# Layer 0's chain to the output weights in two streams by head group, and score fills in the 64x64 tile shape

## The chip, the core and the metric

The kernel runs on one core of a Trainium2 chip. The core has a matrix engine (TensorE, PE in the profile; its weight loads are the row PEld), VectorE (DVE), ScalarE (ACT), GpSimd (POOL) and SyncE (SP, which issues nearly all DMAs here). Each engine works through its own instructions in order and waits on semaphores for the others. The metric is the device time of one execution in microseconds (us); less is better. The profile is one execution taken by the hardware profiler.

## What is computed

Sixteen images of 64x64 positions and 256 channels go through two layers, each of which adds to `x` a function of its group norm. Layer 0 is a linear attention with eight heads of 32, layer 1 an attention over a 7x7 neighbourhood with eight heads of 32 and position embeddings.

```python
def _L0_conv_ref(x, w_qkv, w_out):
    q, k, v = to_heads(split(x @ w_qkv))            # 8 heads of 32, n = 4096 positions
    q = softmax(q, over the head's 32) * 32 ** -0.5
    k = softmax(k, over the n positions)
    context = einsum('bhdn,bhen->bhde', k, v)
    out = einsum('bhde,bhdn->bhen', context, q)
    return out @ w_out

def _L1_conv_ref(x, Wq, bq, Wk, bk, Wv, bv, emb0, emb1):
    q, k, v = x @ Wq + bq, x @ Wk + bk, x @ Wv + bv
    kp, vp = 7x7 neighbourhoods of k (plus embeddings) and of v, zeros outside
    attn = softmax(einsum('bhwnd,bhwndk->bhwnk', q, kp))
    return einsum('bhwndk,bhwnk->bhwnd', vp, attn)

x = x + _L0_conv_ref(_gn(x), ...)
x = x + _L1_conv_ref(_gn(x), ...)
```

## The kernel before

All is float32; a float32 matmul goes through PE in two passes and stands as two records in the profile. One image follows the other. The instruction order of PE, ACT, DVE and SP is written out by hand: an engine does its work in the order in which the Python code issues it, and semaphore waits are derived from which tiles an instruction reads and writes. POOL's instructions are placed by the framework.

PSUM, where matmuls write, is held as two double banks `double[0]`, `double[1]` (pd in the profile) and four single banks `single[0]` to `single[3]` (ps).

**Layer 0** (`layer0`, one call per image; its first three steps run at the end of the image before). The positions are cut into 16 blocks `p` of 256 positions, two rows `t` of 128 each.

- `queries_keys(p)` multiplies normalised positions with the query and key weights into a double bank (L588), takes the exponential of all with ACT (L592, tile `eq`), sums the queries of a head with DVE (L595, L597) and divides them with POOL (L598).
- `context(p)` multiplies the exponential of the keys with the raw positions and a column of ones (L606), for both head groups `hg` of four heads, and sums over all 16 blocks in `pc[hg]`, which is `single[hg]`: 256 columns of sums, and the keys' own sum in column 256.
- `turned(p)` transposes the divided queries with DVE into `qv` (L619, two instructions per block).

The loop issues block `p`'s `queries_keys`, then `context(p - 1)`, then `turned(p - 2)`. After the loop comes **the chain** from the contexts to the output weights, for both groups at once: DVE divides and centres the sums into `cc` (reciprocal L644, L645); the transposes of block 15 follow on DVE; PE transposes `cc` into `other[0]`, which is `single[2]` (L653); DVE scales it by the norm's factor into `cT` (L658, two of 128x256); PE multiplies with the value weights into `other[1]`, which is `single[3]` (L663, in 128x32 tiles); DVE scales the product into `ch` (L670); PE multiplies with the output weights into both double banks (L674, in 32x128 tiles); DVE copies the keys' sums out of `pc` (`z`, L682); DVE (L685, two of 128x512) and ACT (L686) copy the output weights to `w4` in SBUF. Then the output matmuls (L709) read `w4` and `qv`: for each of two channel halves, eight strips in four groups of two. The first group writes `single[0]` to `single[3]`, columns 0 to 255, the second the double banks, and so on in turn. A group `i` reads the queries of blocks `4 * i` to `4 * i + 3`. DVE adds each result to `x` (L726, L723) and takes statistics (L522).

**Layer 1** (`local_attention`): eight passes `k` over a head group and a strip of columns (`SEQUENCE`), each in five steps `g` of two row chunks `c`, 40 steps per image. In a step, `scores` multiplies queries and keys in 64x64 tiles (L967) into one of the double banks per chunk, ACT takes the exponential (L976, L979), and in the next step the products with the values follow (L1011). The two double banks alternate, so the scores of a chunk wait for the exponential of the chunk before the last. `blank` (L944) fills the parts of the double bank that no score matmul writes with a large negative number, by four matmuls of bfloat16 constants; it runs for chunks 0 and 1 of passes 0 and 4 alone, that is in steps 0 and 20. Between the steps run jobs that make keys and queries: a matmul into a single bank (L879), then its evacuation by ACT (L755) or DVE (L757).

Of the kernel before, what the change touches and what calls it, by code (L numbers as in the profile page):

```python
# [14 lines left out]
ALU = mybir.AluOpType  # L15
# [4 lines left out]
P = 128  # L20
W = 64
C = 256
# [11 lines left out]
SCALE = HD**-0.5  # L34
# [397 lines left out]
def attention_fast(tc, io, ok):  # L432


    nc = tc.nc
    with ExitStack() as ctx:
# [3 lines left out]
        double = [ps.tile([P, 2, 512], F32, tag=f"pd{i}", name=f"pd{i}") for i in range(2)]  # L440
# [19 lines left out]
        n = Net(tc, cp, io)  # L460
# [19 lines left out]
        bits = cp.tile([P, 2], BF16, tag="bits", name="bits")  # L480
# [16 lines left out]
        def work_tile(name):  # L497
            return work.tile([P, 1024], F32, tag="work", name=name)

        def watch(total, x, w):  # L500
            nc.gpsimd.tensor_tensor(total[:, :w], total[:, :w], x, ALU.add)  # L501
# [10 lines left out]
        def tokens_of(q):  # L512
            return vbuf[q % 2][:, : 8 * (C + 1)].rearrange("p (t c) -> p t c", c=C + 1)

        def load_tokens(b, q, t0=0, t1=8):

            t = tokens_of(q)
            nc.gpsimd.memset(t[:, t0:t1, C : C + 1], 1.0)
            nc.sync.dma_start(t[:, t0:t1, :C], xt[b, q, :, t0:t1])
# [7 lines left out]
        def normalise(xn, x, mean, rstd, s):  # L527
            for k in range(2):
                n.normalise(xn[k][:, strip(s)], x[k][:, strip(s)], mean, rstd, k)
# [42 lines left out]
        def layer0(b, x, xn, mean, rstd, ready, midway=None):  # L572

            mu = None
            pc, other = single[:2], single[2:]
            eq = {}
# [23 lines left out]
                watch(others, z.rearrange("p t h -> p (t h)"), 2 * HEADS)  # L600
                return e

            def context(p):
                for t in range(2):
                    for hg in range(2):
                        nc.tensor.matmul(  # L606
                            pc[hg][:, : C + 1],
                            eq[p][:, t, C + hg * P : C + (hg + 1) * P],
                            tokens_of(p // 4)[:, 2 * (p % 4) + t],
                            start=(p == 0 and t == 0),  # L610
                            stop=(p == 15 and t == 1),
                        )

            def turned(p):

                e = eq.pop(p)
                for t in range(2):
                    T = 2 * p + t
                    nc.vector.transpose(qv[:, :, HD * T : HD * T + HD], e[:, t, :C].rearrange("p (h d) -> p h d", d=HD))  # L619

            for p in range(16 + 1):
                if p < 16:
                    if p % 2 == 0 and p // 2 + 1 < NS and p // 2 + 1 >= ready:
                        normalise(xn, x, mean, rstd, ORDER[p // 2 + 1])
                    eq[p] = queries_keys(p)
                    if p < 3:
                        yield
                if p == 1:
                    mu = n.spread(mean, lambda name: other[1], small, f"{b}")
                if 1 <= p <= 16:  # L630
                    context(p - 1)
                    q = (p - 1) // 4 + 2
                    if q < 4:
                        load_tokens(b, q, 2 * ((p - 1) % 4), 2 * ((p - 1) % 4) + 2)
                if p >= 2:
                    turned(p - 2)
                if p == 9 and midway:
                    fill()

            r = small.tile([P, 2, 1], F32, tag="krz", name=f"krz{b}")  # L640
            z = small.tile([P, 2, 1], F32, tag="kz", name=f"kz{b}")
            cc = work_tile(f"cc{b}")[:, : 2 * C].rearrange("p (a c) -> p a c", c=C)
            for hg in range(2):
                nc.vector.reciprocal(r[:, hg], pc[hg][:, C : C + 1])  # L644
                nc.vector.scalar_tensor_tensor(cc[:, hg], pc[hg][:, :C], r[:, hg], mu, ALU.mult, ALU.subtract)  # L645
            turned(15)


            ct = work_tile(f"ct{b}")
            cT, ch = ct[:, :512].rearrange("p (a c) -> p a c", c=P), ct[:, 512:768]  # L650
            for hg in range(2):
                for k in range(2):
                    nc.tensor.transpose(  # L653
                        other[0][:, (2 * k + hg) * P : (2 * k + hg + 1) * P], cc[:, hg, k * P : (k + 1) * P], n.ident
                    )
            for k in range(2):
                dst = cT[:, 2 * k : 2 * k + 2].rearrange("p a b -> p (a b)")
                nc.vector.tensor_scalar(dst, other[0][:, k * C : (k + 1) * C], rstd[:, k : k + 1], None, ALU.mult)  # L658
            for hg in range(2):
                for k in range(2):  # L660
                    for h in range(4):
                        rows = slice(HD * h, HD * h + HD)
                        nc.tensor.matmul(  # L663
                            other[1][rows, hg * P : (hg + 1) * P].rearrange("p (a d) -> p a d", a=4),
                            n.wqkv_sb[:, k, 2 * C + hg * P + HD * h : 2 * C + hg * P + HD * h + HD],
                            cT[:, 2 * k + hg, rows].unsqueeze(1).to_broadcast([P, 4, HD]),
                            start=(k == 0),
                            stop=(k == 1),
                        )
            nc.vector.tensor_scalar(ch, other[1][:, :C], SCALE, None, ALU.mult)  # L670
            for hg in range(2):
                for h in range(4):
                    rows = slice(HD * h, HD * h + HD)
                    nc.tensor.matmul(  # L674
                        double[h // 2][:, h % 2, hg * C : (hg + 1) * C],
                        ch[rows, hg * P : (hg + 1) * P],
                        n.wout_sb[rows, hg],
                        start=True,
                        stop=True,
                    )  # L680
            for hg in range(2):
                nc.vector.tensor_copy(z[:, hg], pc[hg][:, C : C + 1])  # L682
            w4 = vbuf[0][:, : 8 * C].rearrange("p (h g c) -> p h g c", h=4, g=2)
            for h in range(2):
                nc.vector.tensor_copy(w4[:, h].rearrange("p g c -> p (g c)"), double[0][:, h])  # L685
            nc.scalar.copy(w4[:, 2:4].rearrange("p h g c -> p h (g c)"), double[1])  # L686
            watch(tops, r.rearrange("p a b -> p (a b)"), 2)
            watch(others, z.rearrange("p a b -> p (a b)"), 2)

# [5 lines left out]
            for co in range(2):  # L695
                for i in range(NS // 2):
# [4 lines left out]
                    for h in range(4):  # L701
# [4 lines left out]
                        for hg in range(2):  # L706
                            for a in range(4):
                                rows = slice(HD * a, HD * a + HD)
# [215 lines left out]
        def local_attention(b, x, y, after_scores, read, beside, between, stored):  # L924
# [9 lines left out]
            def blank(hg, pair):  # L934
                for i in range(2):
                    for e in range(2):
                        rows = slice(32 * (2 * i + e), 32 * (2 * i + e) + 32)
                        to = pair[64 * e : 64 * e + 64, i]
                        if hg == 0:
                            to = to.rearrange("p (a w) -> p a w", w=16)[:, :, 8 - 8 * e : 10 - 8 * e]  # L940
                        else:
                            to = to.rearrange("p (a n) -> p a n", a=2)[:, :, 128 - 128 * e : 160 - 128 * e]
                        one = bits[rows, 1:].to_broadcast([32, 64])
                        nc.tensor.matmul(to, nb[rows, :64], one, start=True, stop=True)  # L944

            def scores(k, c):
                hg, t = SEQUENCE[k]
                ps = psum2()
                if k % 4 == 0 and c < 2:
                    blank(hg, ps)  # L950
# [137 lines left out]
            groups = [(k, g) for k in range(8) for g in range(5)]  # L1088
            held, late, before, kept = None, None, None, []
            rs = {}  # L1090
            for step in range(len(groups) + 2):
                new = None
                place(step, FIRST)
                if step < len(groups):
                    k, g = groups[step]
# [5 lines left out]
                if held:  # L1101
                    k, g, es = held
# [11 lines left out]
                if late:  # L1114
                    k, g, es = late
# [5 lines left out]
                if held:  # L1121
                    k, g, es = held
# [4 lines left out]
                if late:  # L1127
                    k, g, es = late
# [16 lines left out]
        with tc.manual_schedule(engines=ORDERED):  # L1145
# [32 lines left out]
            def completed(steps):  # L1178
                while True:
                    try:  # L1180
                        next(steps)
                    except StopIteration as end:
                        return end.value

            lower = layer0(0, x, xn, *gn, 2, midway)
            for b in range(B):
                more = b + 1 < B
                x, xn = halves(b)
                mean, rstd, chain = completed(lower)
# [503 lines left out]
```

## Time and profile before

| | us |
|---|---|
| median of 3 runs | 5272.87 |
| lowest and highest run | 5268.64, 5277.87 |
| profiled execution, its own time | 5278.82 |
| span of its profile | 5276.9 |

The mean granted clock of TensorE is 0.993. The profile is read by groups of instructions and by timeline: a row gives the start, the length, the engine, the line, the operation with its output and inputs (buffer numbers left out), the shape, how many instructions are merged in it, and in brackets the idle time of its engine just before it and who ended it. In the whole execution the groups of the chain and of the fills are:

```profile
L653 PE MATMUL ps<-ident,cc 128*128 128x128 f32 x64 | 14.0, 300 | 13.7 <-DVE cc L645 13.7
L663 PE MATMUL ps<-ct,wqkv 128*32 128x128 f32 x512 | 21.4, 293 | 9.7 <-DVE ct L658 9.7
L674 PE MATMUL pd<-wout,ct 32*128 32x256 f32 x256 | 22.0, 466 | 8.7 <-DVE ct L670 8.7
L709 PE MATMUL ps<-qq,vbuf 32*128 32x256 f32 x4096 | 247.3, 388 | 12.5 <-DVE vbuf L685 12.5
L944 PE MATMUL pd<-bits,nb 32*64 32x64 bf16 x256 | 14.2, 212 | 0.0
```

Here the columns after the bar are the busy time in us, the mean length of one in ns, and the engine's idle time before them in us with what ended it.

### The profile page before, as it was taken

The numbers are of one execution on the slowest core, as the hardware profiler recorded it, in microseconds if no ns is written. First come the engines' busy times: TensorE is split into PE (matmuls) and PEld (weight loads), VectorE is DVE, ScalarE is ACT, GpSimd is POOL, SyncE is SP. The second block draws the span as 40 slices with busy tenths as digits, with TensorE's granted clock in tenths as the row PEclk, the third lists the DMA queues.
The fourth block names the chain that finished last, engine by engine and source line by source line (L and its number), as shares of the span: only waits on it lengthen the run. The fifth ranks groups of instructions, "written<-read, shape, count | busy, mean of one in ns | idle before, by whom it ended". The sixth has DMA issues, their size and how long they took to land. (4 is left out here: it accounts for less than half of the span.)

```text
span 5276.9 us, 175070 instructions
## 1 busy us (share of the span) xinstructions
PE 5114.0 (97%) x76273; PEld 3770.1 (71%) x76273; DVE 2902.3 (55%) x5610; ACT 2629.5 (50%) x3569; POOL 1444.7 (27%) x2630
## 2 busy tenths in 40 slices
PE   7999999999999999999999999999999999999998
PEld 4776767777676776767767677676776767767676
DVE  5464555646546465464655646555465554745545
ACT  1552736527265372653726537174471744727346
POOL 3141231412314123140331403314032140422404
PEclk9999999999999999999999999999999999999999
DMA  5542625436154351543516445164441634417243
GB/s 134 124 119 51 146 64 128 116 56 150 52 131 115 71 135 49 131 117 72 131 49 135 115 80 134 42 138 107 93 122 43 148 95 103 123 43 150 82 92 88
DMA packets 763657, 537.33 MB, mean 102 GB/s; under 512 B 260656, under 2 KB 701616, under 8 KB 761200
## 3 DMA queue, kind: packets, MB, share of 16 engines
q1 hardware_dynamic: 721664, 515.94, 41.1%
q10 hardware_dynamic: 41216, 10.10, 1.2%
q8 instruction: 602, 9.86, 0.8%
q14 instruction: 175, 1.43, 0.1%
HBM read 367.11 MB, written 158.73 MB: 100 GB/s over the span
## 5 line engine op out<-in xcount | busy, mean ns | idle before, releaser
L996 DVE TENSOR_TENSOR e<-e,e 128x384 f32<-128x384 f32 x1024 | 684.3, 698 | 841.5 <-PE ps L1011 364.9
L755 ACT ACTIVATE qq<-ps,bias 32x512 f32<-32x512 f32 (+1 forms) x960 | 699.9, 734 | 812.5 <-DVE bias L750 657.5
L588 PE MATMUL pd<-wqkv,img 128*128 128x512 f32 x2048 | 926.6, 595 | 8.3 <-DVE img L359 8.3
L967 PE MATMUL pd<-qq,kaug 64*64 64x112 f32 (+5 forms) x24192 | 775.4, 267 | 44.0 <-issue 27.4
L967 PEld LDWEIGHTS pd<-qq,kaug 64*64 64x64 f32 x24192 | 673.3, 133 | 180.4 <-issue 92.7
L592 ACT ACTIVATE eq<-pd 128x1024 f32<-128x1024 f32 x256 | 261.9, 1023 | 1063.0 <-PE pd L588 1063.0
L501 POOL TENSOR_TENSOR others<-others,turn 128x9 f32<-128x9 f32 (+2 forms) x384 | 86.5, 225 | 2185.1 <-DVE turn L1056 2184.3
L588 PEld LDWEIGHTS pd<-wqkv,img 128*128 128x128 f32 x2048 | 387.4, 190 | 393.9 <-issue 350.5
L755 ACT ACTIVATE kaug<-ps,bias 32x512 f32<-32x512 f32 (+1 forms) x864 | 554.8, 651 | 181.2 <-PE ps L879 78.0
L979 ACT ACTIVATE e<-pd 128x896 f32<-128x896 f32 (+2 forms) x576 | 465.5, 835 | 227.8 <-PE pd L967 172.6
L595 DVE TENSOR_REDUCE qz<-eq 128x16 f32<-128x512 f32 x256 | 175.6, 686 | 706.5 <-ACT eq L592 706.5
L976 ACT ACTIVATE e<-pd 128x896 f32<-128x896 f32 (+2 forms) x576 | 463.5, 833 | 168.1 <-PE pd L967 114.8
L1011 PE MATMUL ps<-e,vbuf 128*32 128x112 f32 (+1 forms) x18432 | 529.7, 252 | 12.8 <-issue 12.8
L879 PE MATMUL ps<-img,wqn 128*128 128x160 f32 (+2 forms) x3072 | 536.3, 324 | 0.0
L879 PEld LDWEIGHTS ps<-img,wqn 128*128 128x128 f32 x3072 | 472.1, 190 | 55.9 <-DVE r L1063 10.5
L879 PE MATMUL ps<-img,w 128*128 128x512 f32 x1024 | 501.0, 614 | 0.8 <-DVE qq L757 0.3
L1085 POOL TENSOR_TENSOR img<-img,r 128x320 f32<-128x320 f32 (+1 forms) x512 | 489.1, 980 | 5.0
L606 PEld LDWEIGHTS ps<-vbuf,eq 128*128 128x128 f32 x2048 | 386.4, 190 | 144.7 <-issue 99.9
L1011 PEld LDWEIGHTS ps<-e,vbuf 128*32 128x32 f32 x18432 | 388.3, 110 | 140.7 <-issue 103.3
L606 PE MATMUL ps<-vbuf,eq 128*128 128x257 f32 x2048 | 485.1, 381 | 0.0
L831 PE MATMUL pd<-wvn,img 128*128 128x256 f32 x2048 | 468.1, 382 | 4.0 <-DVE hve L354 4.0
L831 PEld LDWEIGHTS pd<-wvn,img 128*128 128x128 f32 x2048 | 383.0, 190 | 67.7 <-issue 15.3
(142 smaller groups left out, 5577.7 us busy)
## 6 DMA issues: line engine op xcount, KB each, us to landing
vbuf<-vpad SPq DMA_DIRECT2D x1152, 96.0 KB
out<-img SPq DMA_DIRECT2D x256, 256.0 KB
vpad<-v SPq DMA_DIRECT2D x112, 512.0 KB
vbuf<-in_xt SPq DMA_DIRECT2D x158, 256.0 KB
img<-in_xc SPq DMA_DIRECT2D x75, 512.0 KB
img<-in_xc SPq DMA_DIRECT2D x106, 256.0 KB
qq<-pos SPq DMA_DIRECT2D x192, 128.0 KB
vbuf<-in_xt SPq DMA_DIRECT2D x60, 384.0 KB
```

Of the source, the lines that this page charges most:

```text
L588: nc.tensor.matmul(ps[:, t], xn[k][:, n0 : n0 + P], n.wqkv_sb[:, k, : 2 * C], start=(k == 0), stop=(k == 1))
L592: nc.scalar.activation(e, ps, AF.Exp)
L606: nc.tensor.matmul(pc[hg][:, : C + 1], eq[p][:, t, C + hg * P : C + (hg + 1) * P], tokens_of(p // 4)[:, 2 * (p % 4) + t], start=(p == 0 an ...
L755: nc.scalar.activation(dst, src, AF.Identity, bias=bias)
L831: nc.tensor.matmul(pi[:, t], x[k][:, n0 : n0 + P], wv[:, k], start=(k == 0 and t == 0), stop=(k == 1 and t == 1))
L879: nc.tensor.matmul(dst, (wq if what == "q" else wk)[:, k, hg * P : (hg + 1) * P], part(x[k]), start=(k == 0 and i == 0), stop=(k == 1 and ...
L967: nc.tensor.matmul(to, kaug[pl][rows, u, 8 * c : 8 * c + 8].rearrange("p r w -> p (r w)"), q, start=True, stop=True,)
L976: nc.scalar.activation(e.rearrange("p (a n) -> p a n", a=2), ps[:, :, : 2 * m], AF.Exp)
L979: nc.scalar.activation(e.rearrange("p (x r) -> p x r", r=hi - lo), src, AF.Exp)
L996: nc.vector.tensor_tensor(part, part, rows_of(hg, c - 1, before, r0, 8 * c), ALU.add)
L1011: nc.tensor.matmul(dst, stationary, pr, **flags)
L1085: nc.gpsimd.tensor_tensor(yv, xv, by_rows(add[:, :, a - w0 : e - w0], xv), ALU.add)
```

## The change

In the chain, each step is split by head group, and the two groups' steps are issued in turn. The contexts of blocks 14 and 15 are issued first for group 0, then for group 1. The transposed sums of group 1 go to `double[0]`, and the value products of group 1 to `single[2]`, so that each group has banks of its own. Scaling and `ch` become instructions of 128 columns: four and two instead of two and one of 256. The transposes of blocks 14 and 15 and the two copies of the keys' sums are issued behind the copies of the output weights. The dictionary of exponential tiles keeps its entries.

In `blank`, the four matmuls take 64 rows of constants instead of 32 and so stand in 64x64 tiles; the value that they write is twice as large.

```diff
-            def context(p):
+            def context(p, groups=(0, 1)):
                 for t in range(2):
-                    for hg in range(2):
+                    for hg in groups:
...
-                e = eq.pop(p)
+                e = eq[p]
...
-                    context(p - 1)
+                    context(p - 1, (0,) if p >= 15 else (0, 1))
...
-                if p >= 2:
+                if 2 <= p < 16:
                     turned(p - 2)
...
+            context(14, (1,))
+            context(15, (1,))
...
-            for hg in range(2):
+            flipped = other[0], double[0][:, 0]
+            products = other[1], other[0]
+
+            def centred(hg):
                 nc.vector.reciprocal(r[:, hg], pc[hg][:, C : C + 1])
                 nc.vector.scalar_tensor_tensor(cc[:, hg], pc[hg][:, :C], r[:, hg], mu, ALU.mult, ALU.subtract)
-            turned(15)
+            def flip(hg):
                 for k in range(2):
+                    nc.tensor.transpose(flipped[hg][:, k * P : (k + 1) * P], cc[:, hg, k * P : (k + 1) * P], n.ident)
+            def scaled(hg):
+                for k in range(2):
+                    nc.vector.tensor_scalar(
+                        cT[:, 2 * k + hg], flipped[hg][:, k * P : (k + 1) * P], rstd[:, k : k + 1], None, ALU.mult
                     )
-            for k in range(2):
-                dst = cT[:, 2 * k : 2 * k + 2].rearrange("p a b -> p (a b)")
-                nc.vector.tensor_scalar(dst, other[0][:, k * C : (k + 1) * C], rstd[:, k : k + 1], None, ALU.mult)
-            for hg in range(2):
+            def valued(hg):
...
-            nc.vector.tensor_scalar(ch, other[1][:, :C], SCALE, None, ALU.mult)
-            for hg in range(2):
+            def weights(hg):
...
-            for hg in range(2):
-                nc.vector.tensor_copy(z[:, hg], pc[hg][:, C : C + 1])
+            centred(0)
+            flip(0)
+            centred(1)
+            scaled(0)
+            flip(1)
+            valued(0)
+            scaled(1)
+            nc.vector.tensor_scalar(ch[:, :P], products[0][:, :P], SCALE, None, ALU.mult)
+            valued(1)
+            weights(0)
+            nc.vector.tensor_scalar(ch[:, P:], products[1][:, :P], SCALE, None, ALU.mult)
+            weights(1)
             w4 = vbuf[0][:, : 8 * C].rearrange("p (h g c) -> p h g c", h=4, g=2)
             for h in range(2):
                 nc.vector.tensor_copy(w4[:, h].rearrange("p g c -> p (g c)"), double[0][:, h])
             nc.scalar.copy(w4[:, 2:4].rearrange("p h g c -> p h (g c)"), double[1])
+            turned(14)
+            turned(15)
+            for hg in range(2):
+                nc.vector.tensor_copy(z[:, hg], pc[hg][:, C : C + 1])
...
-                        rows = slice(32 * (2 * i + e), 32 * (2 * i + e) + 32)
+                        rows = slice(64 * i, 64 * i + 64)
...
-                        one = bits[rows, 1:].to_broadcast([32, 64])
+                        one = bits[rows, 1:].to_broadcast([64, 64])
                         nc.tensor.matmul(to, nb[rows, :64], one, start=True, stop=True)
```

More of the change, by code (lines that the diff above doesn't have):

```diff
@@ L642, in layer0 @@
             cc = work_tile(f"cc{b}")[:, : 2 * C].rearrange("p (a c) -> p a c", c=C)
-            for hg in range(2):
+            ct = work_tile(f"ct{b}")
+            cT, ch = ct[:, :512].rearrange("p (a c) -> p a c", c=P), ct[:, 512:768]
+            flipped = other[0], double[0][:, 0]
+            products = other[1], other[0]
+            def centred(hg):
                 nc.vector.reciprocal(r[:, hg], pc[hg][:, C : C + 1])
                 nc.vector.scalar_tensor_tensor(cc[:, hg], pc[hg][:, :C], r[:, hg], mu, ALU.mult, ALU.subtract)
-            turned(15)
-            ct = work_tile(f"ct{b}")
-            cT, ch = ct[:, :512].rearrange("p (a c) -> p a c", c=P), ct[:, 512:768]
-            for hg in range(2):
+            def flip(hg):
                 for k in range(2):
-                    nc.tensor.transpose(
-                        other[0][:, (2 * k + hg) * P : (2 * k + hg + 1) * P], cc[:, hg, k * P : (k + 1) * P], n.ident
-                    )
-            for k in range(2):
-                dst = cT[:, 2 * k : 2 * k + 2].rearrange("p a b -> p (a b)")
-                nc.vector.tensor_scalar(dst, other[0][:, k * C : (k + 1) * C], rstd[:, k : k + 1], None, ALU.mult)
-            for hg in range(2):
+                    nc.tensor.transpose(flipped[hg][:, k * P : (k + 1) * P], cc[:, hg, k * P : (k + 1) * P], n.ident)
[3 more added lines that the diff above has]
+                        cT[:, 2 * k + hg], flipped[hg][:, k * P : (k + 1) * P], rstd[:, k : k + 1], None, ALU.mult
+                    )
+            def valued(hg):
                 for k in range(2):
@@ L663, in layer0 @@
                         nc.tensor.matmul(
-                            other[1][rows, hg * P : (hg + 1) * P].rearrange("p (a d) -> p a d", a=4),
+                            products[hg][rows, :P].rearrange("p (a d) -> p a d", a=4),
                             n.wqkv_sb[:, k, 2 * C + hg * P + HD * h : 2 * C + hg * P + HD * h + HD],
@@ L680, in layer0 @@
                     )
-            for hg in range(2):
-                nc.vector.tensor_copy(z[:, hg], pc[hg][:, C : C + 1])
+            centred(0)
[10 more added lines that the diff above has]
+            weights(1)
             w4 = vbuf[0][:, : 8 * C].rearrange("p (h g c) -> p h g c", h=4, g=2)
```

## The prediction

> **What bounds the kernel.** I read the page first, then the list of groups by line, the timeline of one image, the list of TensorE's waits, and the windows table with its granted clock.
>
> ```profile
> PE 5114.0 (97%) x76273; PEld 3770.1 (71%) x76273; DVE 2902.3 (55%) x5610; ACT 2629.5 (50%) x3569; POOL 1444.7 (27%) x2630
> ```
>
> PE is busy 97% of the span and no other engine passes 55%. The chain of waits holds only the last store and says nothing here. So a change counts by what it does to PE's idle time or PE's own work, 16 times (once per image, about 327 us each). PE sits idle some 10 us per image (5277 less 5114, over 16), 2.77 us of it in the stretch that the change rewrites. Timeline of the second image (start, length, engine, line):
>
> ```profile
> 446.85 3.63 PE L606 MATMUL ps<-vbuf,eq 128*128 128x257 f32 x16
> 447.10 1.02 ACT L592 ACTIVATE eq<-pd 128x1024 f32<-128x1024 f32 x1 [4.15 <-PE pd L588]
> 449.18 1.36 DVE L619 STREAM_TRANSPOSE qq<-eq 128x256 f32<-128x256 f32 x4
> ...
> 451.17 0.44 PE L653 MATMUL ps<-ident,cc 128*128 128x128 f32 x2 [0.68 <-DVE cc L645]
> 451.76 0.44 PE L653 MATMUL ps<-ident,cc 128*128 128x128 f32 x2 [0.15 <-DVE cc L645]
> 452.80 1.25 PE L663 MATMUL ps<-ct,wqkv 128*32 128x128 f32 x32 [0.61 <-DVE ct L658]
> 454.46 0.21 DVE L682 COPY kz<-ps 128x1 f32<-128x1 f32 x2
> 454.60 1.15 PE L674 MATMUL pd<-wout,ct 32*128 32x256 f32 x16 [0.55 <-DVE ct L670]
> 455.78 1.29 DVE L685 COPY vbuf<-pd 128x512 f32<-128x512 f32 x2 [1.10 <-PE pd L674]
> 456.53 0.71 PE L709 MATMUL ps<-qq,vbuf 32*128 32x256 f32 x8 [0.78 <-DVE vbuf L685]
> ```
>
> The reader sees PE waiting for VectorE five times (0.68, 0.15, 0.61, 0.55, 0.78). An f32 matmul stands as two records.
>
> **Part 1, the chain as two streams.** I lay it out on this image's clock. VectorE's result reaches PE 0.05 us later (L645 ends 451.70, L653 starts 451.75), PE's reaches VectorE 0.07 later (L663 ends 454.05, L670 starts 454.12), ACT's reaches PE 0.05 later.
>
> *Contexts.* Group 0 of block 15 now follows directly on group 0 of block 14. That is four records of 0.216, done at 447.71, but the exponential of block 15 (L592) ends at 448.12. Before, eight records stood ahead and covered it. PE waits until 448.17 and shows a weight load that is otherwise hidden (0.11: after a wait the first two record groups of L674 stand 0.32 apart, not 0.216). Everything in PE's queue is 0.57 later: the contexts stop streaming at 450.88, not 450.32.
>
> *Head of the chain.* Block 14's transposes no longer stand ahead of the centring, so VectorE does group 0 at 449.81 to 450.46, beside group 1's contexts. Flip 0 runs without a wait, to 451.10. Group 1's sums are complete at 451.04; reciprocal and centring (0.15, 0.48) end at 451.78; flip 1 is 451.83 to 452.27. Of a 128x128 scaling the trace has no row; from 0.150 for one column (L354), 0.191 for 32 (L204) and 0.425 for 256 (L670) I estimate 0.29. Two of them, overlapping 0.08, end at 452.84; the value products of their second half at 453.32; the last `ch` at 453.68; the last weights (0.32 + 0.39) at 454.44. Group 0's steps lie inside these gaps. L674 ended at 455.75, so the head gains 1.31 us, the new context wait included.
>
> *Tail.* What went off the head comes back here. Ahead of the first output matmul (L709) VectorE now does the two copies (454.48 to 455.77), four transposes that were behind the contexts and flips (1.36), and the two z copies, which end at 457.12 and 457.19. Does L709 wait for all that? It needs the transposes only three groups later (blocks 14 and 15 are in its fourth group). But L709 writes columns 0 to 255 of the banks whose column 256 the z copies read. By addresses nothing overlaps, L709 would start after the first copy at 455.23, and the part would bring 16 x 1.30 = 21 us. [...] The changed program's list of waits settles it: its first output matmul waits for the first z copy, the next for the second; before, the first waited for the first L685 copy. So L709 starts at 457.17 and 457.24 against 456.53. PE's last wait is 2.8 us instead of 0.78, and **the part loses about 0.70 us per image, 11.2 in all**; ends 0.5 and 0.9 (8 and 14.4), since the 0.29 enters three times. Behind L709 stands all of PE. ACT's copy and POOL's two additions move with their inputs; POOL's next work is 18 us away. No DMA moves, SP's order is the same, and the kept dictionary entries are no instructions.
>
> **Part 2, the clock.** The windows table (length, busy time of PE, weight loads, VectorE, ACT, POOL, then the granted clock) has a second effect:
>
> ```profile
> 452.26:455.67 3.41, 2.32 (x48) 1.47 (x48) 1.43 (x6) 0.00 (x0) 0.20 (x1) 1.00 0.00 0
> 2080.42:2083.82 3.40, 1.68 (x15) 0.60 (x13) 3.31 (x11) 0.00 (x0) 1.07 (x3) 1.00 0.01 2
> 2083.83:2087.24 3.41, 2.86 (x40) 2.17 (x40) 0.55 (x3) 0.00 (x0) 0.19 (x1) 0.50 0.00 0
> 2090.65:2094.07 3.42, 3.42 (x37) 2.82 (x33) 0.00 (x0) 0.00 (x0) 0.00 (x0) 0.50 0.00 0
> ```
>
> In 4 of 16 images the clock fell to one half in this stretch, for 6.83, 10.24, 6.83 and 10.24 us. All half-clock stretches are multiples of 3.41 us and start on one grid of 3.41 us. From the last context to L709 these images took 7.24, 8.30, 7.42 and 8.01 us, where the other twelve took 6.42 to 6.43; with half of the cold time after L709's start (2.1, 2.6, 1.6, 2.65) that is **14.2 us in this execution**.
>
> [...] I counted PE's streaming time per grid window (columns x 0.84 ns, overlaps once): after the first 30 us every window under 39% was followed by half clock, those of 39 to 42% sometimes, none above; and it stays cold until a window is over some 80% busy. [...] Laying that grid over the old stretch at every phase gives a fall in about 23% of images (the trace: 4 of 16). Over the new one, with its gap of 2.8 us, it gives 71% and 1.45 us per image, 23 us in all. **I take 23 - 14 = +9 us**; ends -2 (mostly lucky phases, about 12 us) and +13 (all images, one window each: 16 x 1.7 - 14.2).
>
> **Part 3, the fills.** They were four 32x64 tiles and are now 64x64, like the scores around them. Timeline at an image's first step, then a step without fills:
>
> ```profile
> 535.34 2.75 ACT L755 ACTIVATE kaug<-ps,bias 32x512 f32<-32x512 f32 x4 [2.45 <-PE ps L879]
> 535.38 0.67 PE L967 MATMUL pd<-qq,kaug 64*64 64x64 f32 x24
> 535.98 0.22 PE L944 MATMUL pd<-bits,nb 32*64 32x64 bf16 x4
> 536.13 0.89 PE L967 MATMUL pd<-qq,kaug 64*64 64x112 f32 x24
> ...
> 538.12 1.41 ACT L976 ACTIVATE e<-pd 128x512 f32<-128x512 f32 x2
> ```
>
> ```profile
> 676.90 1.36 PE L967 MATMUL pd<-qq,kaug 64*64 64x64 f32 x48
> ```
>
> From first fill to the next line's first matmul it is 1.727 us with eight fills, 1.288 without: 0.44 per pair of fills, most of it the array running empty at each change of shape (L967 starts 0.09 after the fills stop streaming). In one shape only a wave of 64 columns stays, 0.05 per chunk, so 0.11, and 0.33 are saved. That a bf16 fill between f32 scores runs the array empty anyway is open, so the low end is 0. There are two pairs per image. In step 0 the saving is worth nothing: ACT runs its four L755 from 535.34, which hang on the job before the fills, then two exponentials until 539.53, and the fourth chunk's scores start at 539.58, on ACT's word. In step 20 (618.0) ACT waits for PE, so it counts: 16 x 0.33 = **-5.3 us**, ends 0 and -10.6.
>
> **Sum.** +11.2 + 9 - 5.3 = +14.9. The profiled execution took 5278.8 (span 5276.9), so 5293.7 for one like it; that lies 6 above the median of the runs, 5272.9, from which I forecast **5287** (5287.8, rounded down).
>
> **Rivals.**
> [...]
> - *The z copies do not gate*: L709 at 455.23 gives 5272.9 - 20.8 - 5.3 = 5247. Against: the list of waits.
> - *All goes cold and the fills save nothing*: +11.2 + 13 = +24, or 5297. For it: the gap alone takes 2.8 of 3.41 us.
>
> **Chances.** Forecast 0.44, clock as before 0.28, no gate 0.06, all cold 0.22. A measurement can tell about 0.2%, 10.5 us, from no change. Slower gets 0.38 of the forecast and all cold's 0.22, 0.60; within takes 0.06 of the forecast and 0.27 of the first rival, 0.33; faster 0.07. The sum of the low ends (8 - 2 - 10.6) is 5268, of the high ones (14.4 + 13) 5300; I take 5268 to 5301, which leaves out the case without a gate. The forecast's own range is 5281 to 5295.
>
> **What would show it.** PE's wait ahead of the output matmuls about 2.8 us, ended by a z copy; a new wait of about 0.46 at block 15's contexts; last weights some 1.3 us earlier; half clock in 9 to 14 images; fills plus scores 1.40 in both steps, and in step 0 an equally longer wait for ACT. It is wrong if L709 follows the first copy, or if the cold images stay at four or five.

## The result and the profile after

The changed kernel took 5300.35 us (median of 6 runs, 5294.98 to 5304.4), the kernel before 5273.37 beside it (6 runs, 5268.13 to 5277.87): 1.0044 times as long, 95% interval 1.003 to 1.0058. That is 27 us more, where the forecast had 14.9. The profiled execution took 5304.4, its span 5302.5, its mean granted clock 0.991.

First the timeline of the second image in the changed kernel (start, length, engine, line; in brackets the engine's idle time before the row and who ended it):

```profile
450.55 2.87 PE L606 MATMUL ps<-vbuf,eq 128*128 128x257 f32 x12 [0.29 <-ACT eq L592]
...
453.26 0.38 PE L656 MATMUL ps<-ident,cc 128*128 128x128 f32 x2
...
454.20 0.44 PE L656 MATMUL pd<-ident,cc 128*128 128x128 f32 x2 [0.56 <-DVE cc L652]
...
454.57 1.20 PE L668 MATMUL ps<-ct,wqkv 128*32 128x128 f32 x32
...
455.69 1.20 PE L679 MATMUL pd<-wout,ct 32*128 32x256 f32 x16
...
456.93 1.29 DVE L701 COPY vbuf<-pd 128x512 f32<-128x512 f32 x2 [0.80 <-PE pd L679]
...
459.64 1.65 PE L729 MATMUL ps<-qq,vbuf 32*128 32x256 f32 x12 [2.75 <-DVE kz L706]
```

The same stretch with VectorE's rows alone shows what stands between the copies and that last row:

```profile
456.93 1.29 DVE L701 COPY vbuf<-pd 128x512 f32<-128x512 f32 x2 [0.80 <-PE pd L679]
458.13 1.41 DVE L619 STREAM_TRANSPOSE qq<-eq 128x256 f32<-128x256 f32 x4
459.47 0.18 DVE L706 COPY kz<-ps 128x1 f32<-128x1 f32 x2
```

The reader sees the five waits of before turned into three. The one between the flips (L656) has grown from 0.15 to 0.56. The value products and the weights run without one. There is a new one at block 15's contexts: 0.29 in the bracket, but ends of matmuls are modelled, and counted from the starts of the four records ahead, 0.216 apart, it is 0.46. The last one is 2.75, ended by a z copy of L706. From the first context of the row ahead (449.22) to L729 it takes 10.42 us; before it took 9.68 (446.85 to 456.53). In all 16 images, the list of PE's waits gives (us in total, times, longest):

```profile
PE ps L729 <- DVE kz L706: 44.0, 16, 2.8
PE pd L987 <- issue: 35.7, 29, 3.1
...
PE ps L1031 <- issue: 12.8, 7, 2.3
...
PE pd L987 <- ACT e L996: 6.0, 30, 0.2
PE ps L606 <- ACT eq L592: 5.0, 16, 0.6
```

The first line was 12.5 us. Before, the two "issue" lines, waits that no semaphore in the trace ends, and the ACT line were:

```profile
PE pd L967 <- issue: 27.4, 21, 2.7
...
PE ps L1011 <- issue: 12.8, 8, 2.1
...
PE pd L967 <- ACT e L976: 2.8, 14, 0.2
```

Then the windows table (start and end, length, then busy time of PE, weight loads, VectorE, ACT, POOL, then the granted clock), for two windows of 3.41 us (all half-clock stretches of this trace start whole multiples of 3.41 us apart, and these windows stand on that grid):

```profile
456.42:459.83 3.41, 0.66 (x12) 0.26 (x12) 2.73 (x8) 1.01 (x1) 0.10 (x1) 1.00 0.00 0
459.83:463.24 3.41, 3.41 (x36) 3.41 (x39) 0.00 (x0) 0.00 (x0) 0.10 (x1) 0.50 0.00 0
```

PE was busy 0.66 of 3.41 us, and the next window ran at half clock, though it was full of work. This happened in 11 of images 1 to 15 (called cold from here on), where before it was 4, and mostly for one window.

Splitting both spans at the first context, the first output matmul, the first positional product and the first scores of each image gives where the 25.6 us between the two profiled executions come from (own sums of the two traces, us):

| stage, 16 images | before | after | difference |
|---|---|---|---|
| contexts to output matmuls | 160.2 | 167.1 | +6.9 |
| output matmuls | 481.3 | 492.9 | +11.6 |
| from the positional products to the scores | 799.5 | 797.9 | -1.6 |
| attention and the rest of the image | 3726.6 | 3735.0 | +8.4 |

The stretch ahead of the first context has the 0.3 that are missing from the sum. The first two lines hold the chain and the clock together: at full clock the chain is 0.74 longer per image, 11.9 in all. The half clock's extra time in images 1 to 15, taken as what lies over the full-clock length, is 14.1 us before and 20.0 after. Nothing in the forecast explains the last line, which was to be *negative*.

### The profile page after: what moved, and what is told of

Its sections match the earlier page's. It is cut to its first block, busy times and chain, and to the rows that moved or that the text cites. A ratio compares the mean times of both kernels' runs of the same rounds, so it can differ in the third digit from the quotient of the medians.

```text
span 5302.5 us, 175118 instructions
## 1 busy us (share of the span) xinstructions
PE 5113.5 (96%) x76273; PEld 3789.7 (71%) x76273; DVE 2913.0 (55%) x5658; ACT 2631.9 (50%) x3569; POOL 1444.8 (27%) x2630
## 3 DMA queue, kind: packets, MB, share of 16 engines
q1 hardware_dynamic: 721664, 515.94, 40.7%
## 5 line engine op out<-in xcount | busy, mean ns | idle before, releaser
L987 PE MATMUL pd<-qq,kaug 64*64 64x84 f32 (+5 forms) x24192 | 776.1, 268 | 57.4 <-issue 35.7
L987 PEld LDWEIGHTS pd<-qq,kaug 64*64 64x64 f32 x24192 | 675.3, 133 | 196.2 <-issue 101.0
L999 ACT ACTIVATE e<-pd 128x896 f32<-128x896 f32 (+2 forms) x576 | 465.7, 835 | 232.3 <-PE pd L987 177.6
L996 ACT ACTIVATE e<-pd 128x896 f32<-128x896 f32 (+2 forms) x576 | 463.7, 834 | 168.5 <-PE pd L987 116.0
```

What stands on the lines that cost most here:

```text
L987: nc.tensor.matmul(to, kaug[pl][rows, u, 8 * c : 8 * c + 8].rearrange("p r w -> p (r w)"), q, start=True, stop=True,)
L996: nc.scalar.activation(e.rearrange("p (a n) -> p a n", a=2), ps[:, :, : 2 * m], AF.Exp)
L999: nc.scalar.activation(e.rearrange("p (x r) -> p x r", r=hi - lo), src, AF.Exp)
```

## The experiments

Each ratio is to the kernel before on the same chip and has a 95% interval; it is not the quotient of the two medians, from which it differs by up to 0.0016. Diffs are against the changed kernel unless they say otherwise.

### Is the gate on the output matmuls the two z copies?

`e1_z_early` issues the z copies ahead of the copies of the output weights.

```diff
+            for hg in range(2):
+                nc.vector.tensor_copy(z[:, hg], pc[hg][:, C : C + 1])
             w4 = vbuf[0][:, : 8 * C].rearrange("p (h g c) -> p h g c", h=4, g=2)
...
-            for hg in range(2):
-                nc.vector.tensor_copy(z[:, hg], pc[hg][:, C : C + 1])
```

> The changed kernel with the two z copies issued on VectorE ahead of the copies of the output weights, where they stood before; all else as changed. Gate and clock (the forecast's theory): the first output matmul follows the first weight copy, so PE's wait there falls from 2.75 to about 0.78 and the stretch from the last contexts' start to the output matmuls from 10.42 to 8.45 us (before: 9.68); with the long gap gone, half clock in or right behind the chain in 0 to 2 images instead of 11. Time 5300 - 16 x 1.97 - 20 = 5249, ratio to before 0.995. Rival, the split itself loses (the new wait at block 15's contexts, short VectorE instructions) and the gate is a small part: the wait falls but the stretch stays at or above 9.68, time 5270 or more. Rival, the loss is from stalls with no releaser elsewhere (the reordered code): the stretch shrinks, the time stays within 10 of 5300 less 31.

5253.65 us, ratio 0.9966 (0.9953 to 0.9978), faster than both kernels. Its timeline in the second image, PE's rows and then VectorE's:

```profile
453.51 1.20 PE L679 MATMUL pd<-wout,ct 32*128 32x256 f32 x16
455.49 3.74 PE L729 MATMUL ps<-qq,vbuf 32*128 32x256 f32 x64 [0.78 <-DVE vbuf L703]
```

```profile
453.85 0.21 DVE L700 COPY kz<-ps 128x1 f32<-128x1 f32 x2
454.74 1.29 DVE L703 COPY vbuf<-pd 128x512 f32<-128x512 f32 x2 [0.67 <-PE pd L679]
455.94 1.41 DVE L619 STREAM_TRANSPOSE qq<-eq 128x256 f32<-128x256 f32 x4
```

The z copies now fill an idle moment of VectorE, the output matmuls follow the first copy after 0.78 us, and the transposes run beside them. The chain takes 8.46 us, as expected, and no image goes cold there.

`e5_z_mid` puts them between the copies and the transposes.

```diff
+            for hg in range(2):
+                nc.vector.tensor_copy(z[:, hg], pc[hg][:, C : C + 1])
             turned(14)
             turned(15)
-            for hg in range(2):
-                nc.vector.tensor_copy(z[:, hg], pc[hg][:, C : C + 1])
```

> The change with the two z copies between the copies of the output weights and the four transposes: the gate on the output matmuls is left, 1.36 us shorter, the clock's cause (a long stretch in which PE hardly streams) is halved. Theory (gate plus clock): contexts to output matmuls 9.06 us per image where the change has 10.42 and z first has 8.46, at most 2 images at half clock there, 5300 - 22 - 16 = 5262, 0.998 of the kernel before. Rival (half clock goes with the length of the wait in proportion): 5 to 6 images at half clock, 5270, 0.999.

5266.33 us, 0.9984 (0.9971 to 0.9997); the chain 9.12, no image cold. The time alone doesn't decide between the two expectations; the count of cold images does, for the theory. Its line in the list of waits stands between the others, with the same ender:

```profile
PE ps L729 <- DVE kz L704: 23.1, 16, 1.4
```

So the gate is the z copies, and its cost follows from how much VectorE does ahead of them: 44.0, 23.1 and 12.5 us of waiting in three orders of the same instructions.

### What does the clock cost?

`e4_warm` leaves the wait as it is and gives PE something to do in it: three matmuls of 512 columns into a bank that is free there, behind the last output weights. Their result is not used.

```diff
             weights(1)
+            for _ in range(3):
+                nc.tensor.matmul(other[1], n.wqkv_sb[:, 0, :P], n.wqkv_sb[:, 0, :512], start=True, stop=True)
```

> The changed kernel with three more matmuls of 128x512 on PE behind the last output weights, into a bank whose content is overwritten later; they take some 2.6 us of the 2.75 us in which PE waits for the z copies. Nothing else is changed, the gate stays. Theory: the stretch to the output matmuls stays at 10.42 us, the half clock behind it goes from 11 images to 0 to 2, and the time falls by the clock's part, about 20 us, to 5280. Rival, the clock has no part in it (half clock comes at random, some from stalls elsewhere): the time stays at 5300, or rises where the extra matmuls delay the output matmuls.

5286.18 us, 1.0014 (1.0005 to 1.0023). PE's rows:

```profile
452.26 2.84 PE L700 MATMUL ps<-wqkv 128*128 128x512 f32 x6
455.08 1.20 PE L731 MATMUL ps<-qq,vbuf 32*128 32x256 f32 x16
```

Useless work fills the wait to its end; the chain is 10.43 us, not a bit shorter, and all images are warm there: 0 of 15 instead of 11. Against the changed kernel's 1.0044 that is 0.3%, 16 us (some 9 either way, by the two intervals), got back by the clock alone; the changed kernel's trace has 20.0.

### The new wait at the contexts

`e6_z_early_old_contexts` is `e1_z_early` with block 14's contexts of both groups ahead of block 15's again.

```diff
-                    context(p - 1, (0,) if p >= 15 else (0, 1))
+                    context(p - 1, (0,) if p >= 16 else (0, 1))
...
-            context(14, (1,))
             context(15, (1,))
```

> The change with z first, and block 14's contexts again of both groups ahead of block 15's, so that the new wait for block 15's exponential goes. Theory (the context wait is paid in full on PE): no wait there, contexts to output matmuls 8.46 - 0.57 = 7.9 us, 9 us less than with z first alone, 5245, 0.995 of the kernel before. Rival (group 0's centring comes 0.3 us later and the second stream waits for it, so that what the contexts gain is lost at the flips): 8.3 to 8.5 us, 0.9966 as with z first alone.

5244.3 us, 0.9944 (0.9928 to 0.996); the chain 7.89. All of the wait comes back, 0.57 per image (0.46 and a weight load of 0.11): eight records stand again ahead of those that need block 15's exponential. Group 0's sums are ready a little later, but its flip still starts right behind the contexts.

### The chain and the fills, each alone

`e2_fills_only` is the kernel before with the new fills; `e3_chain_only` is the changed kernel with the old ones. The diff of the first, against the kernel before; the second has the reverse, against the changed one:

```diff
-                        rows = slice(32 * (2 * i + e), 32 * (2 * i + e) + 32)
+                        rows = slice(64 * i, 64 * i + 64)
...
-                        one = bits[rows, 1:].to_broadcast([32, 64])
+                        one = bits[rows, 1:].to_broadcast([64, 64])
```

> The kernel before with the fills in the 64x64 shape alone. Theory: the two steps with fills take 1.38 and 1.36 us instead of 1.73; step 20's 0.35 counts, step 0's goes into a longer wait for ScalarE's exponential; 16 x 0.35 = -5.6 us, time 5268, ratio 0.999. Rival, both count: -11 us, 5262. Rival, none does (the fills' saving is lost to waits in step 20 too, or to stalls elsewhere): 5273 or above.

> The changed kernel with the old fills of 32x64 tiles. Theory: the chain's gate and clock carry all the loss and the fills pay back 5.6: time 5306, ratio 1.006. If the fills are what loses (new stalls in the attention's steps): 5290 or less.

Fills only: 5282.69 us, 1.0016 (1.0005 to 1.0026), slower, where 0.999 was expected: a miss, and the theory of the fills as the prediction had it falls. Chain only: 5297.63, 1.0055 (1.0042 to 1.0069), as expected in its ratio (1.006), though by the medians it is 1.0039; 10 images cold, chain 10.43. In fills only the chain is the old one, with 5 images cold.

Yet in its own stage the fills' saving is real. From the first fill to the next line's first matmul, the median over 16 images is 1.727 us before; after, it is 1.362 in step 0 and 1.381 in step 20. Where does it go? In step 0 the 300th matmul record behind the first fill starts 16.10 us after it in both kernels: nothing is left there. In step 20 that record starts after 13.95 us before and 13.61 after, so the saving is still there; at the 500th record it is 21.46 and 21.56, and the saving is gone. ScalarE doesn't take it: PE's longer waits for the exponential (the 32 for L979, now L999) are 16.7 us before and 16.9 after. The "issue" waits do grow. Added up over the attention they are 40.7 us before, 37.9 in chain only, and 48.7 after, 56.3 in fills only (whose profiled execution, 5306.82, is 24 us above its median).

These waits stand at places of one list in PE's stream: at matmul records 3399, 4544, 6321, 9373, 12930 and so on; 27 of the 37 in the changed kernel stand where the kernel before has one too. This is one of them in the changed kernel, some 21 us after step 20 of the fifth image has begun, PE's rows of the timeline:

```profile
1624.29 0.50 PE L987 MATMUL pd<-qq,kaug 64*64 64x64 f32 x13
...
1627.51 1.99 PE L987 MATMUL pd<-qq,kaug 64*64 64x64 f32 x35 [2.72 <-issue]
```

PE stops in the middle of a group of 24 scores, between two matmuls, for 2.72 us and for no semaphore that the trace shows. In the trace of the DMA, the queue q8 ("instruction" on the page, 602 packets of 16 KB) has a packet that starts at 1624.86 and lands at 1626.15, 1.36 us before PE goes on. This is no chance: in the kernel before, all 31 such stalls over 0.15 us in the attention end between 1.27 and 1.63 us after a packet of q8 has landed, in the changed kernel all 37 between 1.25 and 1.83, while packets land some 5.9 us apart. And the places fit: in all 13 traces together, each of the 476 stalls is a whole multiple of 127.08 matmul records away from the others of its trace, to within 1.3 records. The 76,273 matmul records make 600 such pieces, and q8 brought 602 packets. In `e4_warm`, which has 96 records more, the stalls moved with the count of records. So the places stand as far apart as they would if each packet of q8 brought one such piece. I read it so that PE's next instructions are not there yet; no run shows that itself. On this reading there is a theory for the fills: time saved ahead of such a place comes back as a longer stall there.

### Does the saving come back there?

Three more kernels and two repetitions test it. `e7_z_early_old_fills` is `e1_z_early`, and `e8_z_early_old_contexts_old_fills` is `e6_z_early_old_contexts`, each with the old fills.

> The change with z first and the old fills of 32x64 tiles. Theory (what the new fills save in the stage comes back as waits of PE for its own instructions): fills and scores 1.73 us per pair instead of 1.37, PE's waits without a releaser in the attention 38 to 42 us in place of 49, the time equal to that with the new fills or under it, 0.995 to 0.9966. Rival (the saving counts): 5.6 us slower than with the new fills, 0.9977, and the waits without a releaser 49 as there.

> The change with z first, the old order of the contexts and the old fills: the version that both theories call the best. Contexts to output matmuls 7.9 us, waits without a releaser about 40 us, 5240, 0.994 of the kernel before. Where the context wait is worth nothing and the fills' saving counts: 0.9977.

`e7_z_early_old_fills`: 5246.84 us, 0.9953 (0.9938 to 0.9968), waits 35.2. `e8_z_early_old_contexts_old_fills`: 5240.21, 0.9935 (0.9918 to 0.9952), waits 43.7, more than expected and hardly less than the 44.8 of the same kernel with new fills. Both times are as expected of the theory. The rival's 0.9977 lies outside the first interval; for the second, a saving that counts would make 0.9954 of `e6_z_early_old_contexts`' 0.9944, which is only just outside.

`e9_wide_fills` is the sharper test, since it changes neither the number nor the order nor the tile shape of instructions. It is `e6_z_early_old_contexts` with the fills of step 20 longer.

```diff
                         one = bits[rows, 1:].to_broadcast([64, 64])
...
+                        n = 64
+                        if hg:
+                            to, n = pair[64 * e : 64 * e + 64, i], 512
+                        one = bits[rows, 1:].to_broadcast([64, n])
```

> The change with z first and the old order of the contexts; the new fills of step 20 (the second head group's) write all 512 columns of each quarter in place of the 64 that they need, ahead of the scores: as many instructions in the same order, and about 0.38 us more of PE's time per pair (2 chunks x 448 columns x 0.42 ns), so that a pair takes 1.75 us in step 20, as with the old fills, and 1.36 in step 0. Theory (PE runs into the end of its loaded instructions there, and time saved ahead of that point comes back as a wait): the waits without a releaser from 60 to 130 us after an image's first scores fall from 15 to 22 us to about 10, and the time is that with the narrow fills, 5244, 0.9944 of the kernel before, within 3 us. Rival (the waits come with the tile shape of the fills, or are chance): they stay at 15 to 22 us and the time is 6 us longer, 5250, 0.9956.

> The change with z first and the old order of the contexts again, beside the version with wide fills and the one with old fills on the same chip. Theory: waits without a releaser 15 to 22 us in the stretch from 60 to 130 us, 0.9944 of the kernel before, equal to the version with wide fills within 3 us. Rival: those waits differ by chance from profile to profile, and may stand at 10.

> The change with z first, the old order of the contexts and the old fills again. Theory: waits without a releaser about 10 us in the stretch from 60 to 130 us, 0.9935 of the kernel before, equal to or up to 5 us faster than the same with the new fills. Rival (the new fills' saving counts): 5 us slower than those.

In step 20 the wide fills and the narrow ones beside them look like this in PE's timeline (wide first):

```profile
612.60 0.41 PE L966 MATMUL pd<-bits,nb 64*64 64x512 bf16 x4
...
614.28 0.38 PE L1033 MATMUL ps<-e,vbuf 128*32 128x48 f32 x16
```

```profile
617.87 0.22 PE L963 MATMUL pd<-bits,nb 64*64 64x64 bf16 x4
...
619.24 0.38 PE L1030 MATMUL ps<-e,vbuf 128*32 128x48 f32 x16
```

The pair takes 1.68 us with wide fills (614.28 less 612.60), 1.38 with narrow ones (median of 16 images; the 1.75 of the expectation was 0.07 too long), so PE gets 0.30 us more to do, 4.8 over 16 images. Over 2 x 448 columns that is 0.33 ns each. The expectation reckoned with 0.42; in the kernel before, the means of L1022 (512 columns, 387 ns) and L944 (64 columns, 212 ns), in other tile shapes, give 0.39. The times of the three, on one chip: wide 5241.58, 0.9914 (0.9895 to 0.9934); narrow 5243.59, 0.9926 (0.9908 to 0.9944); old 5241.41, 0.9918 (0.9902 to 0.9935). No cost of the extra 4.8 us shows, nor of the old fills' 5.5, but intervals of 9 to 10 us either way can't exclude it. The waits by place, from 13 profiles (us; the time counts from an image's first scores, step 20 starts at about 81; the stretch was chosen on the first profiles and stood fixed for `e9_wide_fills` and the two repetitions):

| fills | from 60 to 130 us | up to 60 us | after 130 us |
|---|---|---|---|
| old, 5 profiles | 11.1, 10.0, 12.1, 8.1, 12.2 | 12.2 to 16.8 | 10.3 to 19.0 |
| new, 7 profiles | 16.2, 16.7, 17.7, 21.7, 22.5, 14.9, 16.9 | 14.5 to 22.2 | 11.4 to 16.4 |
| new, wide in step 20 | 13.0 | 16.5 | 11.3 |

Behind step 20 all seven profiles with new fills lie above all five with old ones (means 18.1 and 10.7), and the wide fills, which differ from the new only in PE's time, bring most of it back. `e10_z_early_old_contexts_again` with 16.9 speaks against chance. In the other two stretches the groups overlap, and so do their sums over the whole attention (35.2 to 47.8 with old fills, 44.8 to 56.3 with new).

The granted clock adds a second part. A profile is one execution, but the clock is on record for every run. Its mean is lower with new fills than with old in all five pairs of kernels that differ in the fills alone:

| old fills, new fills | clock with old | clock with new |
|---|---|---|
| before, `e2_fills_only` | 0.9931 (43 runs) | 0.9920 (22) |
| `e3_chain_only`, changed kernel | 0.9920 (6) | 0.9910 (6) |
| `e7_z_early_old_fills`, `e1_z_early` | 0.9957 (6) | 0.9943 (6) |
| `e8_z_early_old_contexts_old_fills`, `e6_z_early_old_contexts` | 0.9958 (6) | 0.9950 (6) |
| `e11_z_early_old_contexts_old_fills_again`, `e10_z_early_old_contexts_again` | 0.9957 (6) | 0.9948 (6) |

The first pair and the last two were each measured on one chip. With wide fills, on the chip of the last pair, it is 0.9957 (6 runs), as with the old ones. Among the 43 runs of the kernel before, 0.001 less of clock goes with 4.9 us more, so the 0.001 of the fills goes with about as much as they save. The last section shows a stall with half clock behind it.

What remains open: the rise of the waits behind step 20 (7.4) is larger than the saving there (16 x 0.35 = 5.5), and the reason of that was not tried. That PE waits there for its instructions is my reading of the times and places of the packets and of this test of padding; no run changed the loading itself.

## Why the prediction was right, and where it was not

**The chain: right, to 0.04 us per image.** +0.70 per image was forecast, 0.74 came. PE's last wait was to be 2.8, ended by a z copy; it is 2.75, by L706. The head was to gain 1.31: the last weights end at 456.89, on the clock of before (2.37 earlier) at 454.52 against 455.75, so it gained 1.23. The estimate of 0.29 holds for `ch` (L694, L697) and was low for the scalings (L660, 0.34 each), which is the rest. The new wait at block 15's contexts was to be 0.46 and a load of 0.11, and 0.57 came back when it was removed. The rival in which the z copies don't gate is refuted by `e1_z_early` and `e5_z_mid`. The forecast took the gate from the changed program's list of waits, and the traces agree: matmuls into columns 0 to 255 waited for a read of column 256, 44.0 us in all for L706 in the changed kernel and 23.1 for L704 in `e5_z_mid`; with the z copies first, in `e1_z_early`, they waited 12.5 for the first weight copy. These are waits that the program holds, and no run shows what the hardware would do without them.

**The clock: the cause right, the size too large.** The step "23 - 14 = +9 us" held on the count of images (71% forecast, 11 of 15 came) and was high in the cost: 20.0 less 14.1, so +5.9. That is one execution of each; the other pair with these two chains, fills only and chain only, has 18.0 and 18.2. Over all runs the mean granted clock is 0.9931 before and 0.9920 in chain only, which at 4.9 us for 0.001 makes 5.4. The forecast's count of streaming time comes out again in all 13 traces: after the first 30 us, half clock followed every window that streamed for under 37% and none over 45%, and full clock came back only behind windows of 81% or more. Laid over the stretch of `e5_z_mid` at every phase, 39% gives no fall, and none came. In the windows table above PE was busy for 0.66 of 3.41 us, and half clock followed. `e4_warm` shows the cause apart from the chain: the same wait, filled with work, and 16 us less. The case "clock as before" of the chances is out with it and with the 11 images at half clock.

**The fills: the step that failed.** "In step 20 (618.0) ACT waits for PE, so it counts: 16 x 0.33 = -5.3 us." The pair's saving is there, 0.346 to 0.365, and in step 0 it is absorbed as forecast (L987's short waits for L996 go from 14 to 30, and 16 us later nothing is left of it). In step 20 I looked at who waits there, and not at what PE runs into 21 us later. The runs put in its place PE's stalls behind step 20, longer by 7.4 us with the new fills (means 18.1 and 10.7), in which, as I read it, the saving is lost, and a lower clock: fills only, 1.0016 in place of 0.999. Over the five pairs, old to new, the ratio rises by 0.0016, 0.0013, 0.0009 and 0.0008 and falls by 0.0011 (`e3_chain_only` to the changed kernel), 0.0007 or nearly 4 us on average, each with an interval of 0.001 or more either way. So the term is not -5.3 but about +4, not told apart from nothing.

**The sum.** 11.9 + 5.9 + 0 to 4 is 18 to 22, of the 27 measured (16 to 31 by its interval) and of the 25.6 between the profiled executions. In those the last few microseconds stand in the attention, as 2.1 us of one wait for a DMA and, as an estimate, some 3 us of half clock behind stalls (27.3 us at half clock there before, 34.1 after, of which half is lost). Chain only is less well accounted for: 11.9 + 5.9 makes 1.0034, below its interval. The measured 5300.35 lies above the forecast's own range (5281 to 5295) and only 0.65 under the upper end of the whole one. That it came out inside is partly luck: the chain and the clock stayed below their high ends, and the rest came from waits and half clock in the attention, which the forecast did not have. The rival that came nearest in time, "all goes cold and the fills save nothing", 5297, was half right: the fills, yes; all cold, no.

**Faster than both.** With the z copies first and the contexts in the old order, the two streams are worth what they promised: `e8_z_early_old_contexts_old_fills` at 0.9935, and again as `e11_z_early_old_contexts_old_fills_again` at 0.9918; 35 to 41 us less than the kernel before, where the changed one takes 27 more. The fills may stay in either form.

## What to carry to other kernels

When work is moved out of a critical stretch, look at which of the moved instructions touch a bank that the next stage writes: two copies of about 0.13 us, put behind 1.4 us of work that nobody waited for, turned a gain of 1.2 us per image into a loss of 0.7. A wait of PE can cost more than its length: behind the 2.75 us here 11 of 15 images ran at half clock, worth 16 us by `e4_warm`, and a few useless matmuls in the wait tell the two costs apart. A saving in one stage counts only if nothing downstream paces the engine (of the 0.35 us per pair of step 20 nothing was left at the 500th matmul record): look for PE's stalls without a releaser behind it, and give the saved time back, by a longer instruction in place of a short one, to see whether it mattered. Compare the clock of all runs too, since it shows what a few profiles can't.

## What the hardware showed beyond the forecast

PE stalls for no semaphore that the traces show, as I read it for its own instructions: 35 to 56 us per execution in the attention, in stalls of up to 3.8 us, each a multiple of 127.08 matmul records from the next and ended 1.2 to 2.0 us after a 16 KB packet of queue q8 has landed. Half clock can follow such a stall too: in the changed kernel, PE was busy for 1.02 us from 1623.77 to 1627.18, around the stall shown, and the next two windows ran at half clock.

```profile
1623.77:1627.18 3.41, 1.02 (x37) 0.69 (x25) 3.33 (x7) 1.02 (x2) 0.21 (x1) 1.00 1.14 284
1627.18:1630.60 3.42, 3.09 (x52) 2.60 (x53) 0.73 (x2) 1.65 (x3) 0.00 (x0) 0.50 0.86 226
1630.60:1634.01 3.41, 3.41 (x10) 1.06 (x12) 0.08 (x1) 1.11 (x3) 0.00 (x0) 0.50 0.38 109
```

In the window from 1627.18 PE was busy for 3.09 of 3.42 us, and yet another at half clock followed. Busy is not streaming: counted as in the forecast, with twice the time per column at half clock (four matmuls of L729 start 0.427 us behind the four before, at full clock 0.216), this window streamed for 83%. In the 13 traces the windows that were followed by more half clock go up to 83%, those followed by full clock begin at 81%. And the length of a fill says little of its price: eight fills in the shape of their neighbours, at 64 columns, cost 0.09 us per pair over the same scores without fills (1.38 against 1.29), in another shape 0.44; at 512 columns in the shape of their neighbours they cost 0.39.
